# New counts of unread matmuls ahead of the TensorE steps, and open PSUM banks as a place for them

## Chip, cores, metric

One core of one Trainium2 chip runs the whole program. The time is the device time of one execution in microseconds (us); several executions are taken and their median is compared. Engines are named as the profile names them: PE is TensorE, DVE is VectorE, ACT is ScalarE, POOL is GpSimd, SP issues most DMAs.

## What is computed

Inputs: x of 8 x 512 x 1024 floats (8 batches b, 512 rows s, width H = 1024), a vector q (row 1 of `cond_2048`), two 1024 x 1024 weights Wk and Wo, an RMS weight, gamma and beta.

```
block_repr = x.reshape(8, 8, 64, H).sum(axis=2)            # 8 blocks of 64 rows per batch
keys   = block_repr @ Wk.T;  keys = keys / rms(keys) * rms_weight
attn   = softmax(keys @ q)                                 # over the 8 blocks
attended = attn @ block_repr                               # one vector per batch
proj   = attended @ Wo.T                                   # the same for all 512 rows
y      = x + proj
out    = x + layernorm(y) * gamma + beta
```

The kernel applies Wo to the block sums and weighs the results, so that both weights meet the same small matrix. All of x goes through the core once in (16 MB) and once out (16 MB).

## The kernel before

The 8 batches form three groups of 2, 4 and 2 (`GROUPS`). Rows are put 128 to a "row" k, so that there are 32 rows k of 128 x 1024, 8 in group 0, 16 in group 1 and 8 in group 2; two rows make a tile of 1 MB, which is loaded and stored by one DMA. For every group the following happens.

1. Block sums: matmuls with a 0/1 matrix (L578, `block_sums`) add the rows of a group into one PSUM bank, `bs0`, `bs1` or `bs2`. For group 2 they come in four steps, of which the first waits for the last tile of x.
2. DVE transposes the sums into `blkT` (L589). Wk and Wo were transposed on PE at the start (L537, copies L544 on DVE and L546 on ACT).
3. Projection: `project(G, 0)` and `project(G, 1)` (L612) multiply by Wk and Wo. For groups 1 and 2 both results lie in one bank, `kv1` or `kv2`: the keys in columns 0 to 255, the values in columns 256 to 511.
4. Softmax: ACT squares the keys (L699), DVE multiplies them by q (L701), a small matmul adds up (L710, the bank `sums`), and a chain of short DVE and ACT instructions gives the weights `wcol` (L741).
5. ACT weighs the values (L748, `vw`), PE spreads them to all rows (`spread_out`, L761, banks `p`), ACT and DVE copy them to `pb` (L772, L770). PE also makes a small table (`table`, L799 and L800) that ACT copies (L802).
6. For each row k: DVE adds `pb` to x and sums (L870), ACT squares and sums (L886). For each unit of 2 or 4 rows POOL works out the scale (L960 to L973), PE transposes it (`unit`, L983, bank `st`), ACT copies it (L987, `lt`).
7. Results, two rows at a time: DVE writes x times (gamma + deviation) into two PSUM tiles `t` (L999), PE adds the table's part (`results`, L1007), ACT scales and writes the rows back (L1013), SP stores them. The last two rows of all (kind E) are finished by DVE without PSUM (L893, L931).

PSUM has 8 banks: three tiles `t0` to `t2` of two banks each (addressed as half tiles `h0` to `h5` until `set_bits`, L1032), and two single banks `b0` and `b1`, which `bs`, `kv`, `sums`, `st`, `p` and `tab` claim in turn.

Every operation is first added to a planner (class `Plan`) as a step with an engine, a duration, its dependencies and the PSUM slot that it claims or releases. `Plan.order` simulates the engines with these durations, takes due times from the table `RANKS`, and gives the order in which the instructions are written out. There are 112 steps on PE; this text numbers them 0 to 111 in their order.

After that `Plan.fill` goes through the PE steps and puts unread matmuls ahead of some: 128 x 128 zeros times 128 x 512 zeros in bf16 (`unread`, L1148), written into PSUM slots that nobody holds at that point by the planner's times, and read by nobody. How many is worked out from a model of how active PE was in the last 3.41 us, with the constants `FILL_ACT`, `LEAST` and `FORCE`. They are written out just ahead of the step:

```
    for n in order:
        for at in plan.between.get(n, ()):
            unread(*at)
        plan.steps[n]["fn"]()
```

Of the kernel before, what the change touches and what calls it, by code (L numbers as in the profile page):

```python
# [26 lines left out]
P = 128  # L27
# [31 lines left out]
FILL_US = 0.23  # L59
FILL_ACT = 0.213  # L60
FILL_FROM = 0.8
SPAN = 3.41
LEAST = 0.6
FORCE = 0.45
T_SPARE = 0.6
LANES = 8
RANKS = (
# [34 lines left out]
class Plan:  # L102
# [3 lines left out]
    def __init__(self):  # L106
        self.steps = []
        self.seen = {}
        self.slots = {}
        self.at = {}  # L110
        self.held = {}
        self.between = {}

    def add(self, eng, us, due, fn, reads=(), writes=(), claim=None, use=None, release=False, frees=None, mb=0.0, touch=True, port=0):
# [19 lines left out]
        self.steps.append(dict(  # L134
            n=n, eng=eng, us=us, after=after, due=due, fn=fn, deps=deps, mb=mb, claim=claim,
            release=(use or claim[1]) if release else None, frees=frees, port=port,
        ))
        return n
# [101 lines left out]
    def fill(self, eng, pools):  # L240

        mine = sorted((s["n"] for s in self.steps if s["eng"] == eng), key=lambda n: self.start[n])
        done = []
        for a, b in zip([None] + mine, mine):
            t0 = FILL_FROM if a is None else self.start[a] + self.steps[a]["us"]
            t1 = self.start[b]
            if a is not None:
                done.append((self.start[a], max(t0, self.start[a] + 0.01), self.steps[a].get("act", 0.0)))  # L250
            if t1 < FILL_FROM:
                continue
            have = sum(act * max(0.0, min(y, t1) - max(x, t1 - SPAN)) / (y - x) for x, y, act in done)
            short = LEAST * max(min(SPAN, t1 - FILL_FROM), t1 - t0) - have
            k = min(max(0, int(short / FILL_ACT + 0.99)), int((t1 - t0) / FILL_US))
            if not k and a is not None and t1 > 2 * SPAN and have < FORCE * SPAN:
                k = 1
            free = []
            for (p, i), held in sorted(self.held.items()):
                if p in pools and pools[p][0] <= t0 and t1 < pools[p][1]:  # L260
                    if all(h[1] <= t1 or h[0] >= t1 + pools[p][2] for h in held):
                        free.append((max([t0] + [h[1] for h in held if h[1] <= t1]), p, i))
            since = min(free)[0] if free else t1
            k = min(k, max(int((t1 - since) / FILL_US), int(since <= t0)))
            if k and free:
                free = [(p, i) for t, p, i in free if t <= since + 0.3]
                self.between[b] = [free[j % len(free)] for j in range(k)]
                done.append((max(t0, t1 - k * FILL_US), max(t1, t0 + 0.01), k * FILL_ACT))


@with_exitstack
def block_attn_resid_kernel(
# [11 lines left out]
    nc = tc.nc  # L284
# [3 lines left out]
    QU = H // 4  # L288
# [406 lines left out]
    def softmax(G, due):  # L695
        n, g = G["n"], G["g"]
        NB = NBLK * g
        keys, _ = place_of(G, 0)
        add(ACT, (0.37, 0.2), due, lambda: nc.scalar.activation(  # L699
            square[:, :QU], bank(keys)[:, :QU], AF.Square, accum_out=sd[:, 0:1]), reads=[f"kv{n}.0"], writes=["sd0"])  # L700
        add(DVE, (0.46, 0.04), due, lambda: nc.vector.scalar_tensor_tensor(  # L701
            vw3, bank(keys)[:, :QU], 1.0, qw, ALU.mult, ALU.mult, accum_out=sd[:, 1:2]),
            reads=["qw", f"kv{n}.0"] + (["sd0"] if n == 0 else []), writes=["sd1"] + (["kv0.used"] if n == 0 else []))
# [6 lines left out]
        work(0.1, (0.36, 0.1), due, lambda: nc.tensor.matmul(bank(pc)[:, :64], ones.to_broadcast([P, P]), flat(sdd), start=True, stop=True),  # L710
            reads=["sdd", "ones"], claim=("b", pc))
        v, sc, r0, a = cv[:, :NB], cs[:, :NB], c0[:, :NB], ca[:, :NB]
# [39 lines left out]
    def spread_out(G, due):  # L752
# [3 lines left out]
        for i in range(2):  # L756
            def go(i=i):
                lo = slice(64 * i, 64 * i + 64)
                for j in range(2):
# [3 lines left out]
                        start=True, stop=True, tile_position=(64 * i, 0),  # L763
                    )
            work(0.43, (0.6, 0.1), due, go, reads=["vw", f"spread{g}"], claim=("b", names[i]))

            def copy(i=i):
                o = pb[n % 2][:, i * HALF : (i + 1) * HALF]
# [375 lines left out]

    def unread(pool, s):

        o = bp[s] if pool == "b" else tp[s][:, 0, :] if pool == "t" else tp[s // 2][:, s % 2, :]
        nc.tensor.matmul(o, zeros[:, :P], zeros, start=True, stop=True)  # L1148

# [38 lines left out]
```

## Time and profile before

| What | Before |
|---|---|
| time of three executions | 152.26, 152.63 and 152.5 us, median 152.5 us |
| the profiled execution | 153.44 us by its own clock, of which 151.7 us are the span from the first to the last instruction |
| PE busy | 122.1 us (80%), 1145 matmul records |
| DVE busy | 110.1 us (73%) |
| ACT busy | 93.6 us (62%) |
| POOL busy | 47.9 us (32%) |
| unread matmuls (L1148) | 107: 66 into `b`, 41 into `t` |
| mean granted PE clock | 0.943 of full speed |
| HBM | 27.28 MB read, 16.78 MB written, 290 GB/s over the span |

The table comes from the profile's page and its list of cores. Busy time is the union of an engine's instructions. "Granted clock" is the share of its full clock that PE was allowed in a stretch; in this trace it is 1 or 0.5 at any moment. The chain of waits follows the work that ended last back from the end, and names at each step the instruction or the wait that it went through.

### The profile page before, as it was taken

The page shows a single profiled execution, that of the slowest core. Times are in us where ns is not written, and L with a number is a line of the kernel's source. Part 1 is how long each engine was busy: PE and PEld are TensorE (multiplying, and loading weights), DVE is VectorE, ACT ScalarE, POOL GpSimd, SP SyncE. Part 2 cuts the span into 40 slices and gives each one's busy share as a digit, 9 for nine tenths or more (in the row PEclk, how much of TensorE's full clock was granted, in tenths as well). Part 3 has the DMA queues.
Part 4 walks back from the last instruction along what each step waited for, and adds up shares of the span by engine and source line. Part 5 has one row for each costly group of instructions (what it writes and reads, how often), then busy time and mean ns, then how long its engine had stood idle before and what let it go on. Part 6 is the DMA issues. An engine that isn't in the chain of part 4 may idle for free.

```text
span 151.7 us, 3008 instructions
## 1 busy us (share of the span) xinstructions
PE 122.1 (80%) x1145; PEld 64.0 (42%) x1145; DVE 110.1 (73%) x183; ACT 93.6 (62%) x162; POOL 47.9 (32%) x129
## 2 busy tenths in 40 slices
PE   5996895999879987799779549997759999679800
PEld 1654574697546333444264123552233743223200
DVE  0068725353896999627669999996895999989960
ACT  3030333334333997555759966997991999997640
POOL 8888888000000063700000736004204002627000
PEclk9999999999999999999999986999995599999955
DMA  5999999999999910157999920579499656557984
GB/s 175 390 404 433 412 411 403 415 420 418 419 421 419 371 41 0 50 235 259 378 415 387 400 102 0 242 276 285 203 218 244 268 207 279 244 209 307 417 322 168
DMA packets 7951, 44.26 MB, mean 292 GB/s; under 512 B 880, under 2 KB 896, under 8 KB 3968
## 3 DMA queue, kind: packets, MB, share of 16 engines
q1 hardware_dynamic: 7760, 43.00, 71.2%
q0 software_dynamic: 144, 1.05, 3.8%
q8 instruction: 9, 0.15, 0.4%
q14 instruction: 6, 0.05, 0.1%
q10 hardware_dynamic: 32, 0.02, 0.1%
HBM read 27.28 MB, written 16.78 MB: 290 GB/s over the span
## 4 chain that ended last, share of the span: by engine, by line
PE 24%; ACT 14%; DVE 14%; issue 6%; POOL 2%; DVEq 0%; ACTq 0%
ACT square L886 9%; PE b L612 7%; PE t L1007 7%; DVE t L999 6%; ACT x L1013 4%; PE b L761 3%; DVE x L870 2%; PE b L578 2%; DVE wkT L893 2%; DVE x L931 1%; POOL urs L968 1%; PE b L799 1%; PE b L983 1%; PE b L800 1%; POOL stat L973 1%
## 5 line engine op out<-in xcount | busy, mean ns | idle before, releaser
L999 DVE SCALAR_TENSOR_TENSOR t<-gam,ustd,x 128x1024 f32<-128x1024 f32 x30 | 38.0, 1292 | 5.8 <-ACT x L1013 5.6
L870 DVE SCALAR_TENSOR_TENSOR x<-x,pb 128x1024 f32<-128x1024 f32 x32 | 37.6, 1217 | 1.7 <-ACT pb L772 1.6
L1013 ACT ACTIVATE x<-t,urs 128x1024 f32<-128x1024 f32 x30 | 32.1, 1107 | 8.6 <-PE t L1007 6.7
L886 ACT ACTIVATE square<-x,stat 128x1024 bf16<-128x1024 f32 x30 | 34.5, 1149 | 3.9 <-DVE x L870 3.2
L960 POOL TENSOR_SCALAR uv<-ussq 128x4 f32<-128x4 f32 (+1 forms) x8 | 5.4, 674 | 83.4 <-ACT square L886 79.2
L1007 PE MATMUL t<-tab,lt 32*128 32x512 f32 x120 | 22.0, 706 | 2.7 <-ACT lt L987 1.6
L1148 PE MATMUL b<-zeros 128*128 128x512 bf16 x66 | 18.5, 387 | 3.3 <-POOL zeros L433 1.8
L537 PE MATMUL t<-ident,x 128*128 128x128 f32 x128 | 16.5, 281 | 3.1 <-DMA x<-in_L_cond_Wk_dram 2.9
L1148 PEld LDWEIGHTS <-zeros 128*128 128x128 bf16 x107 | 10.2, 101 | 18.7 <-issue 8.0
L537 PEld LDWEIGHTS t<-ident,x 128*128 128x128 f32 x128 | 15.1, 193 | 5.7 <-DMA x<-in_L_cond_Wk_dram 2.4
L544 DVE COPY wkT<-t 128x512 f32<-128x512 f32 x8 | 5.4, 689 | 13.4 <-ACT wkT L546 13.0
L546 ACT COPY wkT<-t 128x512 f32<-128x512 f32 x8 | 4.6, 587 | 16.7 <-PE t L537 8.7
L578 PE MATMUL b<-x,blk 128*32 128x256 f32 x176 | 11.8, 400 | 1.8 <-DMA x<-in_x_dram 1.8
L1148 PE MATMUL t<-zeros 128*128 128x512 bf16 x41 | 12.6, 411 | 0.6 <-DVE wkT L544 0.5
L968 POOL TENSOR_TENSOR urs<-uv,minus_half 128x4 f32<-128x4 f32 (+1 forms) x8 | 12.3, 1544 | 0.7
L612 PE MATMUL b<-wkT,blkT 128*32 128x256 f32 x192 | 11.9, 381 | 0.0
L1007 PEld LDWEIGHTS t<-tab,lt 32*128 32x128 f32 x120 | 6.3, 199 | 11.0 <-DVE t L999 4.2
L544 DVE COPY woT<-t 128x512 f32<-128x512 f32 x8 | 5.3, 689 | 6.0 <-PE t L537 3.5
L612 PE MATMUL b<-woT,blkT 128*32 128x256 f32 x128 | 8.3, 382 | 1.1 <-ACT square L699 1.1
L436 POOL TENSOR_SCALAR_AFFINE_SELECT spread<-spread 32x128 f32<-32x128 f32 x24 | 8.8, 376 | 1.0
L578 PEld LDWEIGHTS b<-x,blk 128*32 128x32 f32 x176 | 5.2, 114 | 8.6 <-issue 4.0
L546 ACT COPY woT<-t 128x512 f32<-128x512 f32 x8 | 4.4, 591 | 6.9 <-PE t L537 4.2
(118 smaller groups left out, 141.1 us busy)
## 6 DMA issues: line engine op xcount, KB each, us to landing
x<-in_x_dram SPq DMA_DIRECT2D x16, 1024.0 KB, 10.6
out_dram<-x SPq DMA_DIRECT2D x14, 1024.0 KB, 4.3
x<-in_L_cond_Wk_dram SPq DMA_DIRECT2D x8, 512.0 KB, 11.4
x<-in_L_cond_Wo_dram SPq DMA_DIRECT2D x8, 512.0 KB, 11.5
wkT<-in_L_cond_ln_beta_dram SPq DMA_DIRECT2D x1, 1024.0 KB, 7.4
wkT<-in_x_dram POOLq DMA_DIRECT2D x1, 1024.0 KB, 12.0
out_dram<-x SPq DMA_DIRECT2D x4, 256.0 KB, 3.3
out_dram<-x SPq DMA_DIRECT2D x2, 512.0 KB, 3.3
```

Source lines behind the costliest of these rows:

```text
L537: nc.tensor.transpose(bank(name)[:, bass.ts(c, P)], xs[s][:, r, 4 * i + c :: HC], ident)
L544: nc.vector.tensor_copy(dst, src)
L546: nc.scalar.copy(dst, src)
L578: nc.tensor.matmul(bank(name)[32 * j : 32 * j + 32, :QU], blk[G["g"]], row[:, bass.ts(j, QU)], start=(i == 0 and k == 0), stop=(i == len(p ...
L612: nc.tensor.matmul(bank(name)[32 * j : 32 * j + 32, at : at + QU], b[:, c, :], wT[which][:, c, bass.ts(j, QU)], start=(opens and c == 0), ...
L870: add(DVE, (1.145, 0.07), due, lambda: nc.vector.scalar_tensor_tensor(x_row(k), x_row(k), 1.0, pb[n], ALU.mult, ALU.add, accum_out=total), ...
L886: add(ACT, (1.16, 0.13), due + 1.3, lambda: nc.scalar.activation(square, x_row(k), AF.Square, bias=total, scale=-float(H), accum_out=ussq[ ...
L968: small(lambda: e.tensor_tensor(rs, v, minus_half.to_broadcast([P, U]), ALU.pow), 0.2 + 0.21 * U, [f"uv{u}", f"uv{u}.a", "minus_half"], [f ...
L999: add(DVE, (1.195, 0.09), due + ROW_US * j, lambda j=j: nc.vector.scalar_tensor_tensor(flat(wide(names[j])), gam, ustd[u][:, r + j : r + j ...
L1007: nc.tensor.matmul(wide(names[j])[:, h, :], lts[i][lo : lo + 32, r // RT, :], tab[G["n"] % NTAB][lo : lo + 32, :], start=False, stop=True, ...
L1013: add(ACT, (1.0, 0.11), due + ROW_US * (RP + j), lambda j=j: nc.scalar.activation(x_row(k + j), flat(wide(names[j])), AF.Identity, scale=u ...
L1148: nc.tensor.matmul(o, zeros[:, :P], zeros, start=True, stop=True)
```

## The change

`Plan.fill` no longer works out the counts. A string `FILLS` holds one character for each of the 112 PE steps, a number to base 36, and `fill` takes it as the count of unread matmuls ahead of that step. `LEAST` goes from 0.6 to 0.7, but the branch that uses it runs only where `FILLS` is empty. `seen_at`, which can hold start and end of steps as a trace showed them, is empty in the kernel as written, so that all times are the planner's.

The place is chosen as before among the slots that nobody holds. A second kind of place is new, called `add`: a bank of which an accumulation is under way. It is used where fewer unread matmuls than the count fit in the time for which a slot is free (`most < k`). For `bs` banks it holds from the second block-sum step to the last of that bank: the zeros are added to the sums. For `kv1` and `kv2` it holds from the step after the small sum (L710) to the second spreading step: there two matmuls of 256 columns stand for one of 512, and they add zeros to the half with the keys.

```diff
+FILLS = (
+    "j000g00006000000000500000000000000000000000103000000000000002121000000000000503k34100000000000020046101008c09618"
+)
...
-        mine = sorted((s["n"] for s in self.steps if s["eng"] == eng), key=lambda n: self.start[n])
+        mine = sorted((s["n"] for s in self.steps if s["eng"] == eng), key=lambda n: (self.start[n], n))
+        when = {n: (self.start[n], self.start[n] + self.steps[n]["us"]) for n in mine}
+        when.update(self.seen_at)
+        counts = dict(zip(mine, (int(c, 36) for c in FILLS))) if FILLS else None
...
+                if u.startswith("bs"):
+                    spans[u] = (spans.get(u, (i, i))[0], i)
...
+            if counts:
+                k = counts[b]
+            elif t1 >= FILL_FROM:
...
+            late = t1 - t0 - (p1 - p0)
+            most = max(int((p1 - since + max(0.0, late)) / FILL_US), int(since <= p0)) if free else 0
+            free = [(p, j) for t, p, j in free if t <= since + 0.3]
+            adds = [("add", u) for u, (lo, hi) in sorted(spans.items()) if lo < i <= hi]
+            if most < k and adds:
+                free = adds
+            elif not counts:
+                k = max(0, min(k, most))
+            if not free:
+                k = 0
...
     def unread(pool, s):
 
+        if pool == "add" and s[:2] == "kv":
+            for _ in range(2):
+                nc.tensor.matmul(bank(s)[:, :QU], zeros[:, :P], zeros[:, :QU], start=False, stop=True, skip_group_check=True)
+            return
+        if pool == "add":
+            nc.tensor.matmul(bank(s), zeros[:, :P], zeros, start=False, stop=True, skip_group_check=True)
+            return
```

Read against the steps, the string says this (steps that had none and get none are left out; "steps" are PE steps in their order):

| step | what it is | before | after |
|---|---|---|---|
| 0 | first transposes of Wk (L537) | 15 | 19 |
| 4 | transposes of Wk, third block of rows (L537) | 16 | 16 |
| 9 | gamma rows (L520) | 4 | 6 |
| 19 | transposes of Wk, last block of rows (L537) | 0 | 5 |
| 43, 45 | second half of Wo's projection, group 0 (L612); its last part (L630) | 0, 0 | 1, 3 |
| 60, 61 | `st1` (L983); last block sums of group 1 (L578) | 0, 1 | 2, 1 |
| 62, 63 | results 6, 7 (L1007); first projection of group 1 (L612) | 0, 0 | 2, 1 |
| 76, 78 | `spread_out` of group 1 (L761); its table (L799) | 4, 1 | 5, 3 |
| 79 | first block sums of group 2 (L578) | 21 | 20 |
| 80, 81, 82 | `st2` (L983); results 10, 11 (L1007); second block sums (L578) | 0, 1, 0 | 3, 4, 1 |
| 95 | last projection of group 2 (L612) | 0 | 2 |
| 98 | `st4` (L983) | 0 | 4 |
| 99, 100 | `spread_out` of group 2, first and second part (L761) | 0, 1 | 6, 1 |
| 102 | table of group 2 (L799) | 0 | 1 |
| 105, 106 | results 22, 23 and 20, 21 (L1007) | 11, 11 | 8, 12 |
| 108, 109 | results 24, 25 and 26, 27 (L1007) | 5, 8 | 9, 6 |
| 110, 111 | `st7` (L983); results 28, 29 (L1007) | 0, 8 | 1, 8 |
| all | | 107 | 150 |

The order of the steps, every other instruction and all DMAs stay as they are.

More of the change, by code (lines that the diff above doesn't have):

```diff
@@ L134, in add @@
         self.steps.append(dict(
-            n=n, eng=eng, us=us, after=after, due=due, fn=fn, deps=deps, mb=mb, claim=claim,
+            n=n, uses=uses, eng=eng, us=us, after=after, due=due, fn=fn, deps=deps, mb=mb, claim=claim,
             release=(use or claim[1]) if release else None, frees=frees, port=port,
@@ L240, in fill @@
     def fill(self, eng, pools):
-        mine = sorted((s["n"] for s in self.steps if s["eng"] == eng), key=lambda n: self.start[n])
-        done = []
-        for a, b in zip([None] + mine, mine):
-            t0 = FILL_FROM if a is None else self.start[a] + self.steps[a]["us"]
-            t1 = self.start[b]
-            if a is not None:
[L250 to L257, printed above, removed]
-            free = []
[L259 to L266, printed above, removed]
@@ new lines, in fill @@
+        mine = sorted((s["n"] for s in self.steps if s["eng"] == eng), key=lambda n: (self.start[n], n))
+        when = {n: (self.start[n], self.start[n] + self.steps[n]["us"]) for n in mine}
+        when.update(self.seen_at)
+        counts = dict(zip(mine, (int(c, 36) for c in FILLS))) if FILLS else None
+        at = {n: i for i, n in enumerate(mine)}
+        spans = {u: (at[lo], at[hi]) for u, (lo, hi) in self.spans.items()}
+        for i, n in enumerate(mine):
+            for u in self.steps[n]["uses"]:
+                if u.startswith("bs"):
+                    spans[u] = (spans.get(u, (i, i))[0], i)
@@ new lines, in fill @@
+        done = []
+        self.counts = []
+        for i, b in enumerate(mine):
+            a = mine[i - 1] if i else None
+            t0 = FILL_FROM if a is None else when[a][1]
+            t1 = when[b][0]
+            if a is not None:
+                done.append((when[a][0], max(t0, when[a][0] + 0.01), self.steps[a].get("act", 0.0)))
+            p0 = FILL_FROM if a is None else self.start[a] + self.steps[a]["us"]
+            p1 = self.start[b]
+            k = 0
+            if counts:
+                k = counts[b]
+            elif t1 >= FILL_FROM:
+                have = sum(act * max(0.0, min(y, t1) - max(x, t1 - SPAN)) / (y - x) for x, y, act in done)
+                short = LEAST * max(min(SPAN, t1 - FILL_FROM), t1 - t0) - have
+                k = max(0, min(int(short / FILL_ACT + 0.99), int((t1 - t0) / FILL_US)))
+                if not k and a is not None and t1 > 2 * SPAN and have < FORCE * SPAN:
+                    k = 1
+            free = []
+            for (p, j), held in sorted(self.held.items()):
+                if p in pools and pools[p][0] <= p0 and p1 < pools[p][1]:
+                    if all(h[1] <= p1 or h[0] >= p1 + pools[p][2] for h in held):
+                        free.append((max([p0] + [h[1] for h in held if h[1] <= p1]), p, j))
+            since = min(free)[0] if free else p1
+            late = t1 - t0 - (p1 - p0)
[7 more added lines that the diff above has]
+            if not free:
+                k = 0
+            if k:
@@ L267, in fill @@
                 self.between[b] = [free[j % len(free)] for j in range(k)]
                 done.append((max(t0, t1 - k * FILL_US), max(t1, t0 + 0.01), k * FILL_ACT))
+            self.counts.append(k)
 @with_exitstack
@@ L711, in softmax @@
             reads=["sdd", "ones"], claim=("b", pc))
+        if n:
+            plan.spans[keys] = [len(plan.steps) - 1]
         v, sc, r0, a = cv[:, :NB], cs[:, :NB], c0[:, :NB], ca[:, :NB]
@@ L765, in spread_out @@
             work(0.43, (0.6, 0.1), due, go, reads=["vw", f"spread{g}"], claim=("b", names[i]))
+            if not i:
+                plan.spans[place_of(G, 1)[0]].append(len(plan.steps) - 1)
             def copy(i=i):
```

4 lines of the change are left out of this document (3 added, 1 removed).

## The prediction, made before the changed kernel was run

> **What bounds the kernel now.** I read the page first, for the shares of the engines and the granted clock.
>
> ```profile
> span 151.7 us, 3008 instructions
> ...
> PE   5996895999879987799779549997759999679800
> ...
> DVE  0068725353896999627669999996895999989960
> ...
> PEclk9999999999999999999999986999995599999955
> ```
>
> A slice is 3.8 us. Up to slice 13 the loads run at about 400 GB/s and PE waits for them now and then; later DVE is the fullest engine, but with holes. The clock of PE falls to half in three places: slices 23 and 24, slices 30 and 31, and at the end, where PE has nothing left to do. So the next view is the chain of waits near the first two.
>
> ```profile
> 89.92 0.38 PE b L1148
> 90.30 2.02 PE t L1007 x8
> 92.32 3.35 PE b L578 x48
> ...
> 103.56 1.04 PE b L612 x16
> 104.61 0.02 issue
> 104.63 0.43 DVE vw L701 x2
> ...
> 112.46 1.13 PE b L761 x4
> 113.59 0.32 PE b L1148
> 113.91 1.84 PE b L761 x4
> 115.75 2.02 PE t L1007 x8
> 117.77 1.15 PE b L799 x2
> ```
>
> Columns: start, length, what. In both throttled places the chain runs through PE without a pause, 89.92 to 104.61 and 112.46 to 122.90, while DVE waits: 1.28 us before L701 at 104.63, 1.60 us before L870 at 116.40. Eight L1007 take 2.02 us here and 1.07 us at full clock (96.11). So the clock is worth time just where it is halved. Third, why it falls: busy time in stretches cut at the clock's changes (length, PE busy, PEld, DVE, ACT, POOL, granted clock, DMA).
>
> ```profile
> 83.33:86.74 3.41, 1.65 (x18) 0.67 (x19) 3.41 (x7) 3.32 (x6) 2.40 (x2) 1.00 0.99 389
> 86.74:90.15 3.41, 1.40 (x29) 0.54 (x21) 3.32 (x5) 3.11 (x6) 1.01 (x4) 1.00 0.45 178
> 90.15:93.57 3.42, 3.42 (x25) 1.15 (x28) 3.07 (x6) 1.17 (x2) 3.16 (x4) 0.50 0.00 0
> ...
> 110.63:114.05 3.42, 1.71 (x12) 0.98 (x7) 3.35 (x8) 3.18 (x8) 0.14 (x1) 1.00 0.99 175
> 114.05:117.46 3.41, 3.41 (x12) 1.30 (x11) 1.81 (x3) 0.59 (x1) 1.66 (x4) 0.50 1.00 243
> ```
>
> Half clock follows a stretch with 1.40 or 1.71 us busy of 3.41. The stretch with 1.65 us, mostly 512-column zeros, kept it. The 1.71 us hold 1.06 us of L761, which fills 64 of 128 rows of the array; at half weight they are 1.2 us. So the border lies between 1.4 and 1.65 us of full-array work. Last, two PE waits:
>
> ```profile
> PE b L761 <- ACT vw L748: 2.6, 2, 1.7
> ...
> PE b L612 <- ACT square L699: 1.1, 1, 1.1
> ```
>
> The second is step 95. It writes the values half of `kv2` and needs nothing of the keys, yet waits for ACT's read of the keys half: reads and writes of one PSUM tile are ordered whichever half they touch.
>
> **The change, part by part.** 43 more unread matmuls at 0.216 us (start to start of L1148 in the run of zeros from 5.0 us) are 9.3 us of PE time, plus 0.1 us where float matmuls follow (L1148 at 113.52, L761 at 113.84). What counts is whether PE would idle there.
>
> *Up to 48 us.* Step 0 gets 4, at half clock (0.427 us, 1.77 to 4.73) at worst +1.7 us; PE then has 1.17 us idle for Wk's DMA at 13.30 and 1.47 us at 26.06. Step 9: +0.43 us, taken up by 0.23 and 1.47 us of DMA waits; step 19: 1.08 us in the 1.47. Step 43: +0.3 us, L630 and L612 end near 44.25, but `vw` (L644, 44.38) waits for DVE's L741, which ends at 44.28. Step 45: 0.65 us in an idle 0.82 us. Cost 0, at most 0.1; without the DMA waits it would be 2.4 us.
>
> *56 to 64 us.* Step 60's first goes to `b1`, which `st1` needs too, and both wait for the copy L682 (57.21): +0.3. Step 62's two wait in `b1` for L987 (59.89), so L1007 goes from 59.94 to 60.37 and step 63 from 61.01 to 61.64. Behind them, PE idles 0.78 us before L983 at 63.73, waiting for POOL. ACT's L1013 and DVE's L999 (62.31) come 0.43 us later; the next L1007 wanted that L999 at 64.72 and started at 65.17. Cost 0. Between -0.15 and +0.15: POOL's L973 took 1.27 us beside L999 and 0.22 us elsewhere.
>
> *Steps 76 to 79.* One more in an idle 0.87 us: 0. Step 78's table is 0.43 us later (the first of the three waited for DVE's L770 before, too), but its copy is due at 87.90 and PE idles 1.76 us for x before 86.19: 0.
>
> *Steps 80 to 82, the first halving.* Three go into `bs2` after 87.2, ended by 87.9, before L983 at 88.56. Four more into `bs2` from 89.07: L1007 starts at 90.03 instead of 90.23, since the one of before stood in `b0` behind L987. Step 82: +0.31. The stretch 86.74 to 90.15 gets 1.3 us more, 2.7 in all, far over the border: full clock. L1007 gains 0.95 us, the first L578 0.35: 0.2 + 0.95 - 0.31 + 0.35 = 1.2 us at PE. The projection at 97.11 also needs `blkT`, which DVE makes in its order; DVE can start 0.35 us earlier (its wait at 93.55) and makes it by 96.0. So L612 gains 1.05 us and L701 with it (103.6; DVE is there at 103.0). **-1.05 us.**
>
> *Steps 95 and 98.* Two in the idle 1.1 us at 104.6, four (eight of 256 columns) in the idle 0.96 us before 110.10: 0. ACT's `vw` reads `kv2` at 111.84, long after: 0.
>
> *Step 99, the new place.* Slots are full, so six go into the keys half of `kv2`. They are written out after `vw`'s read of the other half, so by step 95's row they wait for ACT's L748, as L761 itself does. They cannot fill the idle 1.7 us; they stand behind it, with `spread_out`, `pb` and, over it, DVE's whole last group queued: 6 x 0.216 = **+1.3 us** before L761. No row has 256-column bf16 matmuls with a weight load each; if the load (101 ns) is not hidden, it is 2.5 us. I take 1.3, since the zeros' loads are hidden, and the ends of -1.3 (they run in the gap after all) and 2.5.
>
> *The second halving.* Their 1.3 us also lift the stretch up to L761 over the border. Then the second L761 gains 0.87 us, L1007 0.95, the table 2 (4.2 us at half, 2.2 at 78.0). L761 starts 1.05 - 1.3 = 0.25 us later, `pb` and L870 (116.40) are at -1.05 + 1.3 - 0.87 = **-0.6 us**, L1007's end and ACT's L1013 (117.88) at -1.55 us.
>
> *To the end.* Steps 102 to 111 have their counts in idle stretches (L1007 wanted `lt` at 125.3 and 134.4, L999 at 130.1 and 138.3): 0. From 117.88 ACT has no pause until 137.7 and DVE waits for ACT's L1013 at 119.03, 124.07 and 133.16 (0.25, 0.27, 0.54 us). Those 1.06 us let DVE go from -0.6 to ACT's -1.55. The last DVE work ends at 146.57 and the stores 5.1 us later, both **-1.5 us**.
>
> The profiled execution gave 153.44 us: 151.7 of span and 1.7 around it. With -1.5 it would be 151.9. The median was 0.9 below it, so 152.5 - 1.5 = **151.0 us**.
>
> **A rule against it.** No gap in the PE rows of 80 to 114 us is over 1.8 us, and the clock fell twice there. The Trainium skill (TensorE: Matmul & The Clock Gate, "HAM oscillation") asks only that no idle gap exceed about 3.4 us; by that rule these small gaps are not the cause, unread matmuls would not lift the clock, and the third rival's time follows. The rows speak against the rule. The same page ("What's actually happening") says that the window runs free and does not start with the kernel; the changes of the clock here are 20.48 and 6.83 us apart, 6 and 2 windows of 3.41, and which phase another execution has no run here shows.
>
> **Rivals.**
> 1. *The six do run in the idle gap* (the order is kept by columns). Then -1.05 - 0.87 at L870, -2.85 at ACT, about -2.8 at the end: 149.7 us. Step 95's wait speaks against it. Chance 0.05.
> 2. *The clock still falls near 112 us.* In the 3.41 us that hold the gap before L761, 0.86 us of step 98, 0.5 us of L983 and 0.2 to 0.3 us of a neighbour make about 1.6 us of full-array work, right at the border; the trace's own cut at 114.05 is kinder (the six lie in it) than one at 112. Then nothing of the second halving is saved: -1.05 + 1.3 = +0.25; and if it falls before the six, they and the first L761 cost 1.3 + 0.9 more, and less than the sum is passed on, up to +2. Point: six that start at half clock. With a middle of +1: 153.5 us. Chance 0.22.
> 3. *Unread matmuls do not hold the clock in either place.* Then the costs alone are left, +1.3 for step 99, +0.3 for step 82 less 0.2: 153.9 us. Chance 0.06.
> 4. *The gain is swallowed.* The slices behind DVE's end move 417 and 322 GB/s; if the stores that are queued then set the end and not the last one, an earlier DVE only waits longer for them: 152.5 us. For it: the rate is as high as in the loads. Against it: from 122 to 140 the rate is about 250, so no queue stands. Chance 0.12.
>
> **The numbers.** Forecast 0.55, own range 150.1 to 151.9 (weights hidden or in part, the two places of +-0.15, half of DVE's waits given back). With 0.3% (0.46 us, what a measurement tells from no change): faster 0.55 + 0.05 = 0.60; same 0.12 and 0.04 of rival 2's low end, 0.16; slower the rest of rivals 2 and 3, 0.24. The range from 149.9 takes in nearly all of the forecast and up to 153.6 most of rivals 2 and 4.
>
> **What would show it.** Right: no half clock near 90 and 114; eight L1007 in 1.07 us at 90; L701 near 103.6; the zeros of step 99 starting right after L748, with L761 1.3 us behind; the first L870 of group 2 at 115.8; DVE's three waits for L1013 gone. Wrong: zeros of step 99 in the gap (rival 1), half clock between 111 and 118 (rival 2), half clock behind stretches with over 2 us busy (rival 3), or DVE's end earlier but the span the same (rival 4).

## The result: 1.3% slower, and the profile after

The changed kernel takes 154.94 us (median of 22 executions, 153.56 to 155.63), the kernel before 154.17 us on the same chip (22, 151.42 to 155.71). The ratio is 1.0127, with a 95% interval of 1.0089 to 1.0165; it leaves out executions more than 1.5% above the fastest of their kernel, 12 of the 22 of the kernel before and none of the changed one, so it is larger than the quotient of the two medians, 1.005. The profiled executions gave 154.17 us after and 153.44 us before, both 1.7 us above their spans. The forecast was faster by 1.5 us.

Line numbers after the change: block sums L578 are L608, `project` L612 is L642, `vw` L748 is L780, `spread_out` L761 is L793, x + `pb` L870 is L904, `st` L983 is L1017, results L1007 is L1041, their scaling L1013 is L1047. The unread matmuls L1148 are L1189, those added to `bs` are L1186, the pairs of 256 columns in `kv2` are L1183.

First the page, read as before (busy shares and granted clock in 40 slices, here of 3.8 us):

```profile
span 152.5 us, 3113 instructions
...
PE   5999899999899988999879299998959979799900
...
DVE  0059725353885999647669997996994999999960
...
PEclk9999999999999999999999969999999999999995
```

The clock is halved in one stretch, not two, before the end. Yet the span is 0.7 us longer. The place is slice 23, the first of those before, just behind PE's emptiest one. The stretches cut at the windows of the clock (length, PE busy, PEld, DVE, ACT, POOL, granted clock, DMA share, GB/s) show both places that the prediction spoke of:

```profile
83.66:87.07 3.41, 1.31 (x7) 0.39 (x4) 3.41 (x7) 3.34 (x6) 2.39 (x2) 1.00 0.86 308
87.07:90.49 3.42, 2.80 (x19) 0.87 (x19) 3.33 (x5) 2.86 (x5) 0.99 (x4) 0.50 0.61 256
...
114.05:117.46 3.41, 3.41 (x19) 2.12 (x17) 1.97 (x3) 0.94 (x2) 1.73 (x4) 1.00 0.99 219
117.46:120.87 3.41, 3.41 (x30) 2.13 (x33) 2.67 (x5) 2.73 (x4) 0.00 (x0) 1.00 0.93 332
```

The second place keeps its full clock, as forecast. The first is lost, because PE was busy for only 1.31 us of the window ahead of it. Its timeline (start, length, what, idle time before and its releaser) says why:

```profile
84.59 0.38 PE L1189 MATMUL t<-zeros 128*128 128x512 bf16 x1
87.69 1.93 PE L608 MATMUL b<-x,blk 128*32 128x256 f32 x16 [2.73 <-DMA x<-in_x_dram]
89.56 1.26 PE L1186 MATMUL b<-zeros 128*128 128x512 bf16 x3
```

PE waits 2.73 us for the last tile of x, not 1.76. The tile's first matmuls start at 87.69 instead of 86.19, and run at half clock (1.93 us, before 1.07). The new zeros in `bs2` come behind that wait, too late for this window. The chain of waits now goes through that transfer:

```profile
78.95 8.70 DMA x<-in_x_dram
87.65 0.04 issue
87.69 1.93 PE b L608 x16
...
105.74 0.43 DVE vw L731 x2
...
113.02 0.58 ACT vw L780 x2
113.59 0.04 issue
113.64 1.47 PE b L1183 x12
115.11 1.06 PE b L793 x4
```

The load takes 8.70 us; in the trace before the same load took 7.4 (78.72 to 86.14). The last lines show step 99's six as forecast: twelve matmuls of 256 columns that start with the end of ACT's read and stand ahead of the spreading.

### The profile page after: what moved, and what is told of

The parts are those of the page before. It is cut to its first block, busy times and chain, and to the rows that moved or that the text cites. A ratio compares the mean times of both kernels' runs of the same rounds, so it can differ in the third digit from the quotient of the medians.

```text
span 152.5 us, 3113 instructions
## 1 busy us (share of the span) xinstructions
PE 130.1 (85%) x1198; PEld 67.4 (44%) x1198; DVE 110.1 (72%) x183; ACT 93.9 (62%) x162; POOL 46.7 (31%) x129
## 3 DMA queue, kind: packets, MB, share of 16 engines
q0 software_dynamic: 144, 1.05, 3.9%
## 4 chain that ended last, share of the span: by engine, by line
DVE 18%; PE 18%; ACT 10%; DMA 9%; issue 6%; DVEq 0%; ACTq 0%
PE b L642 8%; DVE t L1033 7%; DVE x L904 6%; DMA x<-in_x_dram 6%; ACT square L920 4%; PE t L1041 4%; ACT x L1047 4%; DMA out_dram<-x 4%; DVE wkT L927 2%; PE b L793 1%; DVE x L965 1%; PE b L608 1%; PE b L1183 1%; PE b L1189 1%; DVE vw L731 1%
## 5 line engine op out<-in xcount | busy, mean ns | idle before, releaser
L904 DVE SCALAR_TENSOR_TENSOR x<-x,pb 128x1024 f32<-128x1024 f32 x32 | 37.7, 1220 | 1.5 <-ACT pb L806 1.3
L1047 ACT ACTIVATE x<-t,urs 128x1024 f32<-128x1024 f32 x30 | 32.2, 1109 | 6.9 <-PE t L1041 6.0
L994 POOL TENSOR_SCALAR uv<-ussq 128x4 f32<-128x4 f32 (+1 forms) x8 | 4.9, 607 | 85.0 <-ACT square L920 81.0
L1189 PE MATMUL b<-zeros 128*128 128x512 bf16 x82 | 23.8, 387 | 4.6 <-POOL zeros L463 1.8
L1189 PEld LDWEIGHTS <-zeros 128*128 128x128 bf16 x133 | 12.6, 100 | 27.6 <-issue 15.9
L1041 PE MATMUL t<-tab,lt 32*128 32x512 f32 x120 | 21.3, 640 | 1.6 <-DVE t L1033 0.9
L1189 PE MATMUL t<-zeros 128*128 128x512 bf16 x51 | 15.7, 408 | 0.8 <-DVE wkT L574 0.5
L608 PE MATMUL b<-x,blk 128*32 128x256 f32 x176 | 12.0, 405 | 2.7 <-DMA x<-in_x_dram 2.7
L642 PE MATMUL b<-wkT,blkT 128*32 128x256 f32 x192 | 11.9, 381 | 0.2 <-ACT lt L1021 0.2
L1002 POOL TENSOR_TENSOR urs<-uv,minus_half 128x4 f32<-128x4 f32 (+1 forms) x8 | 11.4, 1427 | 0.7
L1041 PEld LDWEIGHTS t<-tab,lt 32*128 32x128 f32 x120 | 6.4, 182 | 9.7 <-DVE t L1033 3.0
L642 PE MATMUL b<-woT,blkT 128*32 128x256 f32 x128 | 8.3, 382 | 0.6 <-ACT square L729 0.6
L608 PEld LDWEIGHTS b<-x,blk 128*32 128x32 f32 x176 | 5.2, 114 | 8.1 <-DMA x<-in_x_dram 3.2
```

The costliest lines, as they stand in the source:

```text
L608: nc.tensor.matmul(bank(name)[32 * j : 32 * j + 32, :QU], blk[G["g"]], row[:, bass.ts(j, QU)], start=(i == 0 and k == 0), stop=(i == len(p ...
L642: nc.tensor.matmul(bank(name)[32 * j : 32 * j + 32, at : at + QU], b[:, c, :], wT[which][:, c, bass.ts(j, QU)], start=(opens and c == 0), ...
L904: add(DVE, (1.145, 0.07), due, lambda: nc.vector.scalar_tensor_tensor(x_row(k), x_row(k), 1.0, pb[n], ALU.mult, ALU.add, accum_out=total), ...
L1002: small(lambda: e.tensor_tensor(rs, v, minus_half.to_broadcast([P, U]), ALU.pow), 0.2 + 0.21 * U, [f"uv{u}", f"uv{u}.a", "minus_half"], [f ...
L1041: nc.tensor.matmul(wide(names[j])[:, h, :], lts[i][lo : lo + 32, r // RT, :], tab[G["n"] % NTAB][lo : lo + 32, :], start=False, stop=True, ...
L1047: add(ACT, (1.0, 0.11), due + ROW_US * (RP + j), lambda j=j: nc.scalar.activation(x_row(k + j), flat(wide(names[j])), AF.Identity, scale=u ...
```

## The experiments

All are the changed kernel with another string of counts unless said otherwise; "like before" means the counts of the kernel before, which gives back its program. The diffs list steps with their counts. Each batch has its own executions of the kernel before: median 153.62 us for e1 to e4, 153.39 for e5 to e8, 153.94 for e9 to e12, 154.23 for e13 to e16, 153.59 for e17 and e18. Ratios are to those. They differ by up to 1.0% from the quotients of the medians of all executions, so differences between two versions are given by the medians, and by the ratios too where the two disagree. e5 to e12 ran on one chip, e1 to e4 on another, e13 to e18 on a third.

### Which part costs: e1 to e8

**e1**: the kernel before with the middle steps alone.

```diff
 step   43 45 60 62 63
-        0  0  0  0  0
+        1  3  2  2  1
```

> The counts of before, but steps 43, 45, 60, 62 and 63 as in the changed kernel (1, 3, 2, 2, 1). Theory S (stores): these hold up group 0's results by about 0.8 us, the first stores and so the loads into their slots start about 1 us later, and the last tile of group 2 lands 1.2 to 1.5 us later (before 86.2, changed kernel 87.7); nothing gives it back: 1.0 to 1.5 us slower than before. Rival N (new place): the loss is the six zeros of step 99 behind the read of the values; these steps cost nothing: within 0.3 us of before, the tile lands at 86.2 to 86.5.

Measured: 153.69 us, ratio 1.0096 [1.0045, 1.0147]. By the ratio, steps priced at nothing cost 1%; the medians (153.69 and 153.62) are level, so alone they show little. In the trace the tile lands at 85.81, no later than in the trace of before (86.14), which theory S did not expect, and the clock is half from 87.2 to 94.0 and from 111.1 to 121.3 us.

**e2**: the change without the middle steps.

```diff
 step   43 45 60 62 63
-        1  3  2  2  1
+        0  0  0  0  0
```

> The changed kernel with steps 43, 45, 60, 62 and 63 at 0. Theory S: the tile lands at 86.2 to 86.5 again, the projection of group 2 and the clock near 90 and 114 gain as forecast: 0.7 to 1.5 us faster than before, 1.5 to 2.5 us faster than the changed kernel. Rival N: still 0.5 to 1.5 us slower than before, as the changed kernel is.

Measured: 154.18 us, 1.0067 [1.0026, 1.0109]. It gives back only part, and the last tile lands at 87.91, where theory S had 86.2 to 86.5.

**e3**: the kernel before with the new place alone.

```diff
 step   98 99
-        0  0
+        4  6
```

> The counts of before, but steps 98 and 99 as in the changed kernel (4, 6): the new place alone. Theory S: the six stand 1.5 us behind the read of the values, but the clock stays full from 114 to 121 and ACT gets its results about 0.4 us earlier: -0.5 to +0.3 us. Rival N: the wait is not given back, 1.0 to 1.5 us slower than before.

Measured: 152.28 us, 0.9959 [0.9909, 1.0009]; no half clock in its trace until 143 us. By the ratio, any gain is within what can be told from none (the median is 1.3 us under that of before), but the place does not make the change slow.

**e4**: the change without step 99's six.

```diff
 step   99
-        6
+        0
```

> The changed kernel with step 99 at 0 (the four of step 98 stay). Theory S: the tile still lands at 87.5 or later, and the clock may halve near 114 as before: 1 to 2 us slower than before. Rival N: the loss is gone, within 0.5 us of before or faster.

Measured: 155.16 us, 1.0152 [1.0090, 1.0213]. The clock halves again at 116.3; the second L793 takes 2.07 us instead of 1.13. The six are worth about their price here.

**e5**: the kernel before with the early steps alone.

```diff
 step    0  9 19
-       15  4  0
+       19  6  5
```

> The counts of before, but steps 0, 9 and 19 as in the changed kernel (19, 6, 5). Theory E (early steps): the extra zeros at the start run at half clock and hold the second transposes of Wk until about 14.0 us, where the DMA is there at 12.5 to 12.8; the five of step 19 stand where PE has no idle time; DVE's first addition of p (row 0) starts at about 48 instead of 46.5 us, and all that follows is 1.0 to 1.6 us later: 1.0 to 1.6 us slower than before. Theory S (stores) and the forecast: hidden by the waits for Wk, within 0.3 us of before.

Measured: 155.36 us, 1.0119 [1.0054, 1.0185]: slower by somewhat more than theory E had, but not by its way, for DVE's first x + `pb` starts at 46.89 in the trace, not at about 48.

**e6**: the change without them.

```diff
 step    0  9 19
-       19  6  5
+       15  4  0
```

> The changed kernel with steps 0, 9 and 19 as before (15, 4, 0). Theory E: DVE's first addition of p starts at 46.5 to 47 us, 1.0 to 1.6 us faster than the changed kernel, so -0.3 to +0.3 us against before. Theory S: still 0.7 to 1.5 us slower than before, the last tile of group 2 lands late.

Measured: 152.69 us, 0.9920 [0.9865, 0.9974]: 0.7 us under before by the medians, where theory E had 0.3 at most.

**e7**: the change with early and middle steps like before; steps 76 to 111 alone are changed.

```diff
 step    0  9 19 43 45 60 62 63
-       19  6  5  1  3  2  2  1
+       15  4  0  0  0  0  0  0
```

> The changed kernel with steps 0, 9, 19, 43, 45, 60, 62 and 63 as before: only the steps from 76 on are changed. Theory E with what the clock gains: 1.0 to 2.0 us faster than before, the granted clock 0.97 or more. If the late steps themselves cost something: no faster than the new place alone (0.4% faster than before), or slower.

Measured: 150.58 us (150.44 to 151.01), 0.9832 [0.9769, 0.9894]. So the later steps do gain, by 1.7%, and the early and middle ones turn that into a loss. Full clock holds to 142.8 us.

**e8**: the kernel before with the counts around the first halving alone.

```diff
 step   79 80 81 82
-       21  0  1  0
+       20  3  4  1
```

> The counts of before, but steps 79 to 82 as in the changed kernel (20, 3, 4, 1). The forecast's own term for the first halving: 0.5 to 1.2 us faster, no half clock between 87 and 93 us in most executions. If zeros ahead of steps 80 to 82 delay PE more than the clock gives: 0 to 0.6 us slower.

Measured: 152.28 us, 0.9945 [0.9903, 0.9986]. This place gains by itself. In the trace the clock is full until 107.8 us, then half until 118.1.

### The price of single steps: e9 to e12

**e9**: e7 with the changed count of step 0.

```diff
 step    0
-       15
+       19
```

> The kernel with only the steps from 76 on changed (e7), and step 0 at 19 instead of 15. Theory E0 (step 0 is the loss): the second transposes of Wk start 0.9 to 1.7 us later than in e7 (12.7 us) and most of it stays: 0.8 to 1.7 us slower than e7, that is 0.3 to 1.2% faster than before instead of 1.7%. Theory E19 (step 19 is the loss): within 0.3 us of e7.

Measured: 150.91 us, 0.9855 [0.9802, 0.9908]: 0.3 us over e7, hidden as the prediction had it.

**e10**: e7 with the changed counts of steps 9 and 19.

```diff
 step    9 19
-        4  0
+        6  5
```

> e7 with step 9 at 6 and step 19 at 5. Theory E0: the waits for Wk and Wo before 26 us take them up: within 0.4 us of e7. Theory E19: the five stand where PE has no idle time and shift DVE's first addition of p by 0.8 to 1.5 us: 0.8 to 1.7 us slower than e7.

Measured: 153.39 us, 0.9998 [0.9959, 1.0038]: 2.8 us over e7, more than either theory had. PE's timelines of e7 and then e10, at Wo's first transposes:

```profile
20.67 4.21 PE L567 MATMUL t<-ident,x 128*128 128x128 f32 x32
25.88 1.13 PE L567 MATMUL t<-ident,x 128*128 128x128 f32 x8 [1.00 <-DMA x<-in_L_cond_Wo_dram]
```

```profile
21.10 3.23 PE L567 MATMUL t<-ident,x 128*128 128x128 f32 x24
24.38 0.38 PE L1189 MATMUL b<-zeros 128*128 128x512 bf16 x1
24.87 0.81 PE L1189 MATMUL t<-zeros 128*128 128x512 bf16 x3
25.51 1.94 PE L567 MATMUL t<-ident,x 128*128 128x128 f32 x16
```

Step 9's two put PE 0.43 us back (20.67 to 21.10) and step 19's five follow; the 1.00 us wait for Wo holds the one or the other, not both. DVE's first x + `pb` starts at 46.75 instead of 46.31. That is 0.44 us of PE time, yet the last tile is 1.7 us later (86.69, not 84.98), and the clock halves from 87.8 to 91.2, which it does not in e7.

**e11**: e7 with twice the six of step 99.

```diff
 step   99
-        6
+       12
```

> e7 with 12 instead of 6 unread matmuls at step 99, all behind the read of the values. If each stands on the path, as the forecast has it (1.47 us for six by the traces): 1.2 to 1.6 us slower than e7. If the wait is hidden behind DVE and ACT: under 0.4 us slower.

Measured: 152.13 us, 0.9920 [0.9882, 0.9957]: 1.5 us over e7, while the forecast price of six is 1.3. Its timeline:

```profile
110.32 2.78 PE L1183 MATMUL b<-zeros 128*128 128x256 bf16 x24 [1.77 <-ACT vw L780]
113.03 1.13 PE L793 MATMUL b<-vw,spread 64*128 64x256 f32 x4
```

The 24 take 2.71 us from start to start of the next: 0.113 us each, so their weight loads (0.1 us each in the trace of before) are hidden.

**e12**: e7 with four pairs for step 99 written out *ahead of* ACT's read of `kv2`.

```diff
             reads=["wcol", f"kv{G['n']}.1"], writes=["vw"], use=name, release=True)
+        plan.weighed = len(plan.steps) - 1
...
         for at in plan.between.get(n, ()):
             unread(*at)
+        if n == plan.weighed:
+            for _ in range(4):
+                unread("add", "kv2")
```

> e7 with step 99 at 0 and four unread matmuls into the keys half of kv2 written out just before ACT's read of the values, so that they run in the idle time behind st4. By the forecast's price of the wait: spread_out starts 1.4 us earlier against the same read; if the clock stays full, 0.6 to 1.4 us faster than e7. Rival: four are too few, the clock halves near 112 us and the time is 0.5 to 1.5 us slower than e7.

Measured: 149.73 us (149.32 to 150.30), 0.9774 [0.9722, 0.9825]; the fastest version of all, ahead of both kernels. In its timeline the zeros stand in the gap and the spreading follows the read at once:

```profile
108.37 1.05 PE L1184 MATMUL b<-zeros 128*128 128x256 bf16 x8
110.20 1.13 PE L794 MATMUL b<-vw,spread 64*128 64x256 f32 x4 [0.79 <-ACT vw L780]
```

### Why hidden zeros cost 2.8 us: e13 to e18

**e13**: e7 with step 19's count alone.

```diff
 step   19
-        0
+        5
```

> The counts of e7 with 5 ahead of step 19. Theory (one wait used twice): in e7 PE idles 1.00 us for Wo's DMA at 25.88; step 19's zeros (1.08 us) fit into it but for 0.1 us, and it is only with step 9's two (0.43 us) that the sum passes it, which gives the 0.44 us seen in e10. So e13 is within 0.5 us of e7: 150.6 to 151.1 us, ratio 0.983 to 0.987, first x+p of DVE near 46.4, last tile's matmuls near 85.1. Rival (the zeros of step 19 cost by themselves, through the PSUM slots they take from the transposes): nearly all of e10's 2.8 us stays, 152.9 to 153.4 us, first x+p near 46.75.

Measured: 150.75 us, 0.9875 [0.9817, 0.9933]; the theory's number. But its reason is not borne out: in this trace DVE's first x + `pb` is at 46.83, later than e10's 46.75, and nothing is lost by it.

**e14**: e10 with ten more zeros in PE's wait for the last tile.

```diff
 step   79
-       20
+       30
```

> The counts of e10 with 30 instead of 20 ahead of step 79, ten more in PE's wait of 3.07 us for the last tile of x. Theory (of e10's 2.8 us, 1.7 are the later landing and 1.1 the halved clock behind PE's longer wait): the clock stays full at 88 to 91, the keys' product is at 104.0 instead of 105.0, and the time is 1.0 to 1.2 us below e10's: 152.3 us, ratio 0.991 to 0.993. Rival (the clock is lost by another stretch, or the landing alone carries the 2.8 us): 153.4 us, ratio 0.998 to 1.001, half clock near 88 to 91 again.

Measured: 152.04 us, 0.9957 [0.9919, 0.9996]. The clock stays full, as the theory said. By the ratios that is 0.6 us less than e10, by the medians (from two chips) 1.35, so the halved clock is a part of the 2.8 us. The rest is put down to the landing, which e14 leaves as it was: the last of the load's 16 parts comes 1.58 us behind the others, in e10 1.56.

**e15**: e7 with the middle steps of the change (which turned out to be the same string as e6).

```diff
 step   43 45 60 62 63
-        0  0  0  0  0
+        1  3  2  2  1
```

> The counts of e7 with 1, 3, 2, 2, 1 ahead of steps 43, 45, 60, 62, 63. Theory (they cost what they cost alone in e1, through the landing of the last tile and the clock behind it): 1.4 us over e7, 152.0 us, ratio 0.992 to 0.994, last tile's matmuls at 85.9 or later and half clock near 87 to 91. Rival (their price in e1 was the lack of the later zeros, which hold the clock here): within 0.3 us of e7, 150.6 us, ratio 0.981 to 0.985.

Measured: 153.19 us, 1.0004 [0.9948, 1.0059]; with e6 (0.9920) some 0.9 to 1.7% over e7. The middle steps cost about as much as steps 9 and 19, though they lie elsewhere and delay other work. The half clock that the theory had near 87 to 91 is not in e15's trace: it is full until 143.8 us, although PE waits 2.99 us for the tile, and that execution took 152.16 us.

**e16**: e7 without step 99's six.

```diff
 step   99
-        6
+        0
```

> The counts of e7 without the six of step 99, so that PE idles 1.7 us for the weighing of the values with nothing in it. Theory (the zeros are needed there, and e12 shows their right place): the clock halves between 110 and 121, the spreading and the next results take 1.5 to 2 us longer, but the 1.5 us of the zeros' own time are saved: 150.5 to 151.5 us, ratio 0.982 to 0.989, 0.8 to 1.8 us over e12. Rival (step 98's four and the zeros before it are enough): full clock at 110 to 121 and e12's time, 149.7 us, ratio 0.976 to 0.979.

Measured: 151.45 us (149.32 to 152.87), 0.9871 [0.9805, 0.9937]. In its trace the clock halves at 112.7 and eight L1041 take 1.92 us, though that execution itself took only 149.89 us. By the medians zeros are wanted at step 99, best in e12's place.

The traces part by something that none of the theories had named. Of the 16 parts in which the late load lands (the increments of its semaphore), one is late in some kernels and none in others. Beside it stands the start of a 16 KB transfer that the profile lists as queue 8, kind "instruction". In order of the number of unread matmuls up to step 79:

```
kernel   unread up to   fetch in    load: 15th of   16th of   last
         step 79        queue 8     16 parts        16        behind
e8           61          86.77        84.72         84.75      0.03
before       62          89.51        86.12         86.14      0.02
e3           62          88.22        84.92         84.92      0.00
e7           64          88.05        84.78         84.94      0.16
e12          64          88.12        84.89         85.00      0.11
e9           68          89.35        84.80         85.16      0.36
e13          69          88.61        85.40         85.47      0.07
e10          71          83.22        85.08         86.64      1.56
e1           71          82.72        84.96         85.81      0.85
e5           73          82.95        85.32         86.36      1.04
e15          73          82.93        85.62         87.00      1.38
e2           75          83.88        86.36         87.91      1.55
e14          81          84.12        86.33         87.91      1.58
after        84          82.81        86.53         87.65      1.12
```

The other six kernels fit in: 0.05 to 0.13 us behind for e11 and e16 (64) and e18 (67), with the fetch at 86.9 to 92.6; 1.49 and 1.09 for e6 and e17 (73) and 1.81 for e4 (84), with the fetch at 82.5 to 85.2. So the border lies between 69 and 71.

The transfer is taken to be a refill of PE's own instructions: in the trace of after the nine of queue 8 stand 249 PE records apart on average (164 to 360), no other engine has more than 224 records in the whole trace, and each unread matmul is two records, a weight load and a matmul. The times fit this reading: with up to 69 zeros PE comes to the place where it asks for the refill only after its wait for the last tile; with 71 it comes to it before, and the refill starts while that tile is landing. No view shows the place itself.

A refill is not the only thing that makes a part late. The load behind this one has its last part 1.36 us behind in e16 and 1.30 us in e18, with no instruction transfer while it was under way.

The DMA view of 82 to 86 us, e7 and then e10, shows the refill:

```profile
q1 hardware_dynamic: 215, 1.62, 101.5%
```

```profile
q1 hardware_dynamic: 219, 1.58, 98.6%
q8 instruction: 1, 0.02, 1.4%
```

(Columns: packets, MB, share of 16 engines' time.) The 16 DMA engines are full without it. The last two kernels move the refill on purpose.

**e17**: e7 with two edits that are free by themselves (e9, e13).

```diff
 step    0 19
-       15  0
+       19  5
```

> The counts of e7 with 19 ahead of step 0 and 5 ahead of step 19. Alone, these cost 0.3 us (e9) and 0.2 us (e13). Theory (instruction fetch): PE's stream up to step 79 is then 9 unread matmuls longer than in e7, beyond the border that lies between 5 (e13) and 7 (e10), so the 16 KB fetch in queue 8 comes at 82.5 to 83.5 us instead of 88, one of the 16 parts of the load issued near 77.4 lands 1.2 to 1.7 us behind the others, PE waits about 3 us for the last tile, and the time is 152.5 to 153.5 us, ratio 0.995 to 1.001. Rival (the costs are those of waits and add up): fetch wherever it is, all 16 parts within 0.7 us, 151.1 us, ratio 0.983 to 0.989.

Measured: 152.98 us (151.67 to 154.17), 1.0052 [1.0007, 1.0097], the time as the theory had it, the ratio a little over. The refill is at 82.51, 15 parts land by 84.83 and the last at 85.92, and PE waits:

```profile
85.96 1.36 PE L608 MATMUL b<-x,blk 128*32 128x256 f32 x16 [2.81 <-DMA x<-in_x_dram]
```

0.3 and 0.2 us have become 2.4 (over e7), though DVE's first x + `pb` starts at 46.28, no later than in e7.

**e18**: e10 with four fewer at the start; steps 9 and 19 stay as they were blamed.

```diff
 step    0
-       15
+       11
```

> The counts of e10 (6 ahead of step 9, 5 ahead of step 19) with 11 instead of 15 ahead of step 0: the two edits that cost 2.8 us stay, but PE's stream up to step 79 is only 3 unread matmuls longer than in e7. Theory (instruction fetch): the fetch in queue 8 is back behind the first matmuls of the last tile, at 87 to 89.5 us, the 16 parts of the load land within 0.7 us, and the time is 150.6 to 151.4 us, ratio 0.982 to 0.990. Rival (steps 9 and 19 cost by the 0.44 us that they delay DVE's first x+p): 153 to 153.5 us, ratio 0.998 to 1.002. Were the shorter run of zeros at the start to let the clock fall before 20 us, the first x+p would be late, which would show there.

Measured: 151.24 us (13 executions; twelve between 150.37 and 152.14), 0.9941 [0.9896, 0.9986]. The time is the theory's and 2.15 us less than e10's; the ratio lies between the theory's and the rival's. Against e17, of the same set, it is 1.74 us less by the medians and 1.1% by the ratios. The profiled execution had its clock halved from 14.7 to 21.5 us, so it is some 3.3 us late from there on, and again from 89.8 to 93.2; in it the refill is at 92.6, behind the load, whose 16 parts land within 0.7 us, and PE's wait is back at the length of e7's:

```profile
88.34 1.07 PE L608 MATMUL b<-x,blk 128*32 128x256 f32 x16 [1.88 <-DMA x<-in_x_dram]
```

So the place of the refill is the cause of most of e10's loss: moved forward by harmless edits it costs 2.4 us, and moved back with the blamed edits in place it takes 2.15 of their 2.8 us away (the four zeros saved at step 0, which e9 prices at 0.3 us, included). That the late part and the refill share one DMA engine is inferred from the one late part out of 16; no view names the engine.

## Why the prediction was wrong, point by point

**The step that failed: "Up to 48 us ... Cost 0, at most 0.1", and with it "56 to 64 us ... Cost 0" and "PE idles 1.76 us for x before 86.19".** An unread matmul was priced as PE time only, and for that the waits did hold it (e9 0.3 us, e13 0.2 us). But it is also two instructions that PE must fetch. The 22 more up to step 79 moved a refill from 89.5 to 82.8 us, into the landing of the tile for which PE waits at that moment. The landing, which the sum took as given, was 1.5 us later: its last part came 1.1 us behind the other 15, and those were 0.4 us later than before. PE's gap grew from 1.76 to 2.73 us, and the clock fell behind it.

This does not account for the whole loss. By the medians the changed kernel is 4.4 us over e7, by the ratios 2.9%; e17 shows 2.4 us for the refill, and the early waits have 0.7 at most (below), so over 1 us by the medians stays open. A candidate is another refill in after, at 68.3 us, that has a late part beside it too: 15 parts of the store issued at 64.30 have landed by 68.17, the last at 70.34 (before: all 16 by 67.17, the refill at 67.3), and the next load goes out at 70.36, 6.06 us behind that store instead of 5.64. That place was not tried by itself.

The Trainium skill (Runtime: NRT & Kernel Launch, "Instruction fetch mechanics") says that instructions come in blocks of 16 KiB, 256 of them, over a DMA queue of their own, and that crossing a block is mostly hidden. The size agrees with queue 8 (16384 bytes, 249 records). "Hidden" does not hold for the data beside it: 0.85 to 1.8 us on the last part of the load, 2.4 us on the kernel (e17).

A smaller fault of the same step: step 9's 0.43 us and step 19's 1.08 us were both booked against DMA waits of 0.23 and 1.47 us in the trace of before. In e7's trace, with the same counts up to there, the wait is 1.00 us, and in e10 0.44 us came through: one execution's waits were taken for the program's. By e18 this cost 0.7 us at most (151.24 against e7's 150.58).

**The first halving, -1.05 us,** was right where the landing is undisturbed. From the last tile's first matmul to L701's work on the keys it takes 18.44 us before and 17.3 in e7: -1.1. In after the window ahead of it had lost too much, and it is 18.05. But the halving was one execution's: in e3's trace, with the counts of before up to step 97, the clock does not fall near 90, and the same way takes 17.50 us.

**Six behind ACT's read, +1.3 us,** was right: from the end of the read at 113.59 to the spreading at 115.03 it takes 1.44 us, and twice the six take 2.71. The order is kept for the bank, not for the columns; rival 1 is out. The Trainium skill (PSUM — Partial Sum Buffer, "PSUM bank collisions raise a hardware error") asks for that order, since it counts accesses by bank and quadrant, disjoint columns included; the wait in the trace agrees.

**The second halving, L870 at -0.6 us**: the gain behind the six was there. From the first spreading matmul to group 2's first x + `pb` it takes 3.94 us before and 3.17 after, -0.77 where the sum had -0.87. So rivals 2 and 3 did not happen in the profiled execution of the changed kernel. L904 itself is at 118.20 instead of 116.40: +1.11 by the keys, 0.06 by the softmax, and +0.63 here.

**To the end, -1.5 us**: from that point the span gains another 1.1 us (1.80 late at L904, 0.73 at the end), where the sum had 0.9. Counted from the last tile's first matmul, all later steps together make 65.55 us before and 63.93 in e7: -1.6, the forecast -1.5. In after it is 64.78, and the tile 1.50 us later: +0.7. That -1.6 comes so near to the forecast is partly luck: e3 has 64.18 with steps 98 and 99 alone changed, since its clock did not fall near 90. And by the medians e7 is 2.8 us under the kernel before; its tile comes 1.2 us earlier than in the trace of before, as it does in e3 and e8, which do not differ from before up to there (but for one zero in e8).

**The border between 1.4 and 1.65 us.** As busy time it does not hold elsewhere. The clock fell behind 2.27 us (e5, 107.39 to 110.80) and 2.47 us (e8, 104.39 to 107.81), the sign that the prediction gave for rival 3, and held behind 1.45 us (e9, 83.40 to 86.81). In e5's stretch most of the time is L1041, whose matmuls fill 32 of 128 rows. Weighing by the filled part, as the prediction did with L761, would fit; no run tries it.

**The starting value.** The kernel before had a median of 152.5 us in three executions and 153.4 to 154.2 us in six larger sets. Its executions differ by up to 5.6 us within a set, with the clock's windows lying otherwise in each; the six executions each of e7 and e12, whose clock holds in the trace, stay within 1 us.

**The rule of the Trainium skill weighed in the prediction** (TensorE: Matmul & The Clock Gate, "HAM oscillation": no idle gap over about 3.4 us) is not enough here: the clock fell behind gaps of 2.73 us (after) and 2.81 us (e17), and it held in e7 and e14, with zeros and gaps of 1.79 and 1.16 us. In e15 it held with a gap of 2.99 us, which two of its windows shared (1.68 and 2.17 us busy), so the place of the gap in the windows counts too.

## What to carry to other kernels

Filler work is free only if its time and its instructions are both free: where a transfer is on the critical path, look at when the instruction queues' packets fall, and count the instructions ahead of it before adding more. A wait can hide one insertion; do not book two against it. And filler for a gap must be written out ahead of the access that makes the gap (e12, with four in place of six, 0.85 us better than behind it and the fastest version, 2.3% under the kernel before).

## What the hardware showed that was not expected

- A refill of PE's instructions, 16 KB and 0.9 to 1.0 us of one queue, goes with one of 16 parts of a 1 MB load landing 0.85 to 1.8 us late while the 16 DMA engines are full; two more unread matmuls (69 to 71) decide whether it does.
- 1.1 us of later landing became 2.4 us of time (e17); the longer wait also cost the clock, which is halved from 86.6 to 90.0 there; ten zeros in the wait held it and gave 0.6 to 1.35 us back (e14 against e10).
- All changes of the granted clock in a trace are whole multiples of 3.41 us apart, and their place differs between executions of one program (e6 and e15 are one program: half clock from 27.2 to 30.6 and from 88.6 to 95.4 us in the one, none between 7.3 and 143.8 in the other); e7 and e12, whose clock holds in the trace, have little spread.
